# The first layer's normalization and routing moved in front of the first round of a two-layer recurrent block

## The chip, the cores and the metric

The kernel runs on one core of a Trainium2 chip. The metric is the time of one execution on the device in microseconds (us), median of several runs. The core has a matrix engine (TensorE, PE in the profile), a vector engine (VectorE, DVE), an activation engine (ScalarE, ACT), a general engine (GpSimd, POOL), a queue that issues most transfers (SyncE, SP) and 16 DMA engines. Each engine works through its own list of instructions in order and waits on semaphores for the others. Data lies in SBUF, a memory of 128 partitions; matmul results go to the eight banks of PSUM.

## The reference

x has two sequences of 2048 tokens of 256 numbers. There are two layers, each of the form x + s * silu(g), where s is an attention branch and g a feed-forward branch, both of them computed from the layer-normalized x:

```python
xn = _layernorm(x, axis=-1)
s = _L0_attn_ref(xn, ...)            # local attention of 16 heads, window 128, and 64 pooled latent tokens
g = _silu(_L0_ffn_ref(xn, ...))      # mixture of 8 experts
x = x + s * g
xn = _layernorm(x, axis=-1)
s = _L1_attn_ref(xn, ...)            # a second transformer block
g = _silu(_L1_ffn_ref(xn, ...))      # two layers of rotary local attention with a gated feed-forward
x = x + s * g
```

Only the first layer is touched here, and of it mostly the choice of expert:

```python
router_logits = x @ Wr.T                                   # 4096 x 8
expert_idx = jnp.argmax(jax.nn.softmax(router_logits, axis=-1), axis=-1)
for e in range(E):                                         # E = 8
    mask = (expert_idx == e)[:, None].astype(x.dtype)
    inter = inter + mask * gelu(x @ W1[e] + b1[e])         # 256 -> 1024
y = inter @ Wo + bo + x                                    # 1024 -> 256
out = layernorm(y) * gamma + beta
```

So each token goes to exactly one expert, the one with the largest of its eight logits.

## The kernel before

Tokens lie in 32 tiles of 128, and four tiles make a group, so there are eight groups (`NT` = 32, `GT` = 4, `NG` = 8). Everything is fp32.

**The first layer runs in eight rounds**, one for each group. A round is the attention of its four tiles. Beside it run the projections of the next group (`head(g + 1)`: queries, keys, latent queries and latent keys) and a share of the experts. The function `in_turn` merges such pieces: each piece (a lane) is a list of steps with weights and is given a stretch of the round, (0.05, 0.75) for instance; the steps of all lanes are sorted by their place and issued in that order. The engines keep the order in which the instructions were issued, so this list is the order of work on each engine.

**Normalization and logits: `prep(g)`.** For each tile of the group two DVE instructions find mean and variance (L79, L80). POOL turns them into 1/sqrt(var + eps) (L84, L85). DVE normalizes the four tiles in place (L88). SP stores the rows to DRAM, to `rows_n` (L916), from where the experts will gather them. TensorE transposes the eight 128x128 pieces (L890), DVE and ACT copy the two halves to SBUF (L71, L69), and eight matmuls against the 256x8 router weights give the logits of the four tiles (L898, two passes each). DVE then finds the largest of eight logits for each token as a one-hot row, in five small instructions (L906 to L910). Groups 0 to 3 go in front of round 0, together with `head(0)`; groups 4 to 7 run as lanes inside round 0. The buffers of x are four, so the loads of groups 4 to 7 wait for earlier stores.

**Routing: `route()`**, at 0.48 to 0.6 of round 0. The experts work on tokens sorted by expert, in 39 tiles of 128 places (`FT` = 32 + 8 - 1), each of which belongs to one expert. Two matmuls give each token's rank inside its tile and each tile's count for each expert (L936). `running` sums the counts over the tiles by doubling, ten DVE instructions (L942 to L946). `ends` gives the number of tiles for each expert and their running sum (L955 to L969). `places_of` gives each token's place (L975 to L981), and `tiles_of` splits it into tile and row by comparing with all 40 tile edges (L987 to L995). `experts_of` gives the expert of each of the 39 tiles, as integers `exi` (L1030 to L1034). `tokens_of` inverts the map: for each of the eight groups DVE builds two one-hot operands, `one` and `num` (L1002 to L1013), and four matmuls add them up in one PSUM bank (L1016); from this come the token numbers of every place, `src` (L1024 to L1026).

**Experts.** SP reads each tile's expert number into a register (L1051) and loads that expert's 1 MB of weights, two tiles deep (L1054). POOL gathers the 128 rows of `rows_n` (L1056). TensorE transposes them (L1069), does the first product (L1083), ACT does Gelu (L1092), TensorE the second product with `Wo` (L1100). The result is normalized, scaled and stored sorted (L1115). The list of expert steps is dealt out to the rounds by `shares`: 0.35 for round 0, 1 for rounds 1 to 6, 0.03 for round 7. In round 0 the experts take the last 0.35. The load of `Wo` and of the bias rows and the first expert's weights and rows are issued after routing, when the memory of x is free (`open_experts`).

**Attention.** Scores of one block of 64 queries are made in four banks (L114); DVE adds the mask and finds the row minimum (L107), ACT takes exponentials (L136, and L1245 for the latent part), TensorE transposes (L151) and multiplies with the values (L165). The projections are L204 and L207, L208 (queries), L214, L218 and L220 (keys), L1171 (latent queries), L228 and L236 (values).

The second layer follows and overlaps with the last round; it is the larger part of the time and is not touched.

Of the kernel before, what the change touches and what calls it, by code (L numbers as in the profile page):

```python
# [8 lines left out]
AF = mybir.ActivationFunctionType  # L9
ALU = mybir.AluOpType  # L10
AX = mybir.AxisListType
# [19 lines left out]
def kernel(ctx: ExitStack, tc: tile.TileContext, io: dict, col: dict):  # L31
# [787 lines left out]
    with ExitStack() as l0_ctx:  # L819
# [11 lines left out]
        x_ctx = ExitStack()  # L831
        xp = pool("xp", 1, "right", x_ctx)
        xn = {}

        def load_x(g):
            if g < NG:
                xn[g] = sb(xp, [P, GT, D], "xn", 4)
                nc.sync.dma_start(xn[g], xin[:, g * GT : (g + 1) * GT, :])

        for g in range(4):  # L840
            load_x(g)
            if g == 0:
                wr = sb(l0, [P, 2, E], "wr")
                nc.sync.dma_start(wr, io["WrT"].rearrange("(k p) e -> p k e", p=P))
                wqkv = sb(wa, [P, 2, 3 * D], "wqkv")
                nc.sync.dma_start(wqkv, io["L0_attn_qkv_w"].rearrange("(k p) n -> p k n", p=P))
                rqw = sb(wa, [P, 2, 64], "rqw")
                nc.sync.dma_start(rqw, io["L0_attn_rq_w"].rearrange("(k p) n -> p k n", p=P))
                rkvw = sb(wa, [P, 2, 128], "rkvw")
                nc.sync.dma_start(rkvw, io["L0_attn_rkv_w"].rearrange("(k p) n -> p k n", p=P))  # L850
                halves = load_halves(wa, "halves_a")
            if g == 1:
                routw = sb(wa, [64, 2, P], "routw")
                nc.sync.dma_start(routw, io["a_rout_w"].rearrange("p (e n) -> p e n", e=2))
                outw = sb(wa, [P, 2, D], "outw")
                nc.sync.dma_start(outw, io["a_out_w"].rearrange("(k p) n -> p k n", p=P))
                rows = load_rows(wa, "rows_a")
        cst_a = sb(wa, [P, io["cst_a"].shape[1]], "cst_a")
        nc.sync.dma_start(cst_a, io["cst_a"])
# [4 lines left out]
        edges = cst_a[:, 648 : 649 + FT]  # L864
        starts = edges[:, 0:NT]
        places = cst_a[:, 649 + FT : 649 + 2 * FT]
        along, down = cst_a[:, 649 + 2 * FT : 777 + 2 * FT], cst_a[:, 777 + 2 * FT : 778 + 2 * FT]
# [6 lines left out]

        def prep(g):
# [3 lines left out]
            o = oh[:, g * GT : (g + 1) * GT, :]  # L879

            def moments(t):
                if not t:
                    d["mv"] = sb(xp, [P, GT, 2], "ln_mv", 3)
                    d["rs"] = sb(xp, [P, GT], "ln_rs", 3)
                ln_moments(xp, d["mv"], t, [xn[g][:, t, :]])

# [6 lines left out]
            def logits():  # L893

                lg = d["lg"] = bank("s")[:, 0 : GT * E].rearrange("p (t e) -> p t e", t=GT)
                for t in range(GT):
                    for k in range(2):
                        nc.tensor.matmul(  # L898
                            lg[:, t, :],
# [5 lines left out]
                mx = sb(xp, [P, GT], "mx", 2)  # L905
                nc.vector.tensor_reduce(mx, lg, AX.X, ALU.max)  # L906
                nc.vector.tensor_tensor(o, lg, bc(mx, 2, [P, GT, E]), ALU.is_equal)
                nc.vector.tensor_tensor(o, o, bc(desc, 1, [P, GT, E]), ALU.mult)
                nc.vector.tensor_reduce(mx, o, AX.X, ALU.max)
                nc.vector.tensor_tensor(o, o, bc(mx, 2, [P, GT, E]), ALU.is_equal)  # L910

            lane = [(1, lambda t=t: moments(t)) for t in range(GT)]
            lane += [(1, lambda: ln_rsqrt(d["rs"], d["mv"], 1e-5)), (2, lambda: None)]
            lane += [(1, lambda t=t: normalize(xn[g][:, t, :], xn[g][:, t, :], d["mv"], d["rs"], t)) for t in range(GT)]
            store = rows_n[g * GW : (g + 1) * GW, :].rearrange("(t p) d -> p t d", p=P)
            lane.append((0, lambda: nc.sync.dma_start(store, xn[g])))  # L916
            lane += [(1, lambda c=c: turn(c)) for c in range(2)] + [(1, lambda: None), (1, logits)]
            return lane + [(0, lambda: load_x(g + 4))]

        def route():  # L920

            d = {}
            flat = oh.rearrange("p t e -> p (t e)")

            def two(shape, tag):
                return [sb(xp, shape, f"{tag}{i}") for i in range(2)]

            def ranks():
                ones = sb(xp, [P, P], "ones")
                nc.vector.memset(ones, 1.0)  # L930

                d["rank"] = sb(xp, [P, NT, E], "rank")
                d["total"] = sb(xp, [P, NT, E], "total")
                for name, m in (("rank", before), ("total", ones)):
                    mm = bank("s")[:, 0 : NT * E]
                    nc.tensor.matmul(mm, lhsT=m, rhs=flat, start=True, stop=True)  # L936
                    nc.vector.tensor_copy(d[name].rearrange("p t e -> p (t e)"), mm)

            def running():

                cum = two([P, NT, E], "cum")
                nc.vector.tensor_copy(cum[0], d["total"])  # L942
                k, a = 1, 0
                while k < NT:
                    nc.vector.tensor_copy(cum[1 - a][:, 0:k, :], cum[a][:, 0:k, :])
                    nc.vector.tensor_tensor(  # L946
# [113 lines left out]
        def expert(i):  # L1060
            d = {}

            def begin():
                if i + 1 < FT:
                    expert_load(i + 1)
# [865 lines left out]
```

## Time and profile before

| | us |
|---|---|
| median of 3 runs (lowest, highest) | 2983.13 (2982.27, 2983.95) |
| the profiled execution | 2981.85 |
| its span, first to last instruction | 2980.1 |
| PE busy | 2745.5 (92%) |
| DVE busy | 1900.0 (64%) |
| ACT busy | 1676.8 (56%) |
| POOL busy | 1090.0 (37%) |

The mean clock granted to TensorE is 0.959 of full. In the tables below a row gives a stretch of the span, its length, then for each engine the us in which it was busy and, in brackets, the number of instructions; then the granted clock, the share of time in which the DMA engines were busy and the rate. PEld is the loading of weights into TensorE, which overlaps with its matmuls. In the timeline a row gives start, length, engine, line, operation, output and inputs, and in square brackets how long the engine was idle before it and what ended this. One fp32 matmul shows as two records.

### The profile page before, as it was taken

To read this page: it belongs to the slowest core of one execution; us is meant where nothing else is said; L and a number is where in the kernel's file an instruction comes from. 1 tells how busy PE (TensorE), PEld (TensorE's weight loads), DVE (VectorE), ACT (ScalarE), POOL (GpSimd) and SP (SyncE) were. 2 spreads that over 40 slices of the span, in tenths; PEclk is the share of its full clock that TensorE was granted. 3 is DMA by queue.
4 is the path that set the end of the run, shared out by engine and by line. 5 is a ranking of instruction groups with operands and counts; after the bars stand their busy time and mean duration, and the time that the engine had idled before them with its cause. 6 is when DMAs were issued, how large, how long until landed. Compare 5 with 4: busy or idle time off the path is not lost.

```text
span 2980.1 us, 72390 instructions
## 1 busy us (share of the span) xinstructions
PE 2745.5 (92%) x28226; PEld 1979.7 (66%) x28226; DVE 1900.0 (64%) x6725; ACT 1676.8 (56%) x4587; POOL 1090.0 (37%) x1236
## 2 busy tenths in 40 slices
PE   6789999999987899999999999999998999999997
PEld 4567787787864556656666666666666666666666
DVE  5746655565666877767676777676766555555542
ACT  2347777777764444544444444555554566777672
POOL 1113333333344555555453544443544112222212
PEclk7789999999988999999999999999999999999999
DMA  4032222222211111010000010000001010000000
GB/s 149 24 109 90 81 86 97 82 83 85 92 32 56 62 30 30 23 30 26 16 26 30 16 31 16 5 6 7 5 5 31 18 38 18 28 23 23 15 16 22
DMA packets 84229, 123.57 MB, mean 41 GB/s; under 512 B 7729, under 2 KB 74449, under 8 KB 78897
## 3 DMA queue, kind: packets, MB, share of 16 engines
q1 hardware_dynamic: 80480, 109.64, 11.3%
q0 software_dynamic: 3408, 9.31, 1.1%
q8 instruction: 224, 3.67, 0.5%
q14 instruction: 117, 0.95, 0.1%
HBM read 88.65 MB, written 21.89 MB: 37 GB/s over the span
## 4 chain that ended last, share of the span: by engine, by line
PE 64%; DVE 15%; ACT 11%; issue 5%; POOL 4%; DMA 1%; SPq 0%; POOLq 0%; DVEq 0%; ACTq 0%
PE s L744 10%; PE s L535 5%; PE s L766 4%; PE s L1100 4%; PE tp L151 4%; PE s L1083 3%; PE s L1725 3%; ACT pr L136 3%; PE s L663 3%; ACT pr L1598 3%; PE s L551 2%; PE s L1712 2%; DVE pr L107 2%; PE s L458 2%; PE acc L488 2%
## 5 line engine op out<-in xcount | busy, mean ns | idle before, releaser
L579 POOL TENSOR_TENSOR inv<-inv,nhalf 128x16 f32<-128x16 f32 x64 | 187.2, 2925 | 448.3 <-DVE inv L578 448.1
L107 DVE CUSTOM_DVE_ANT_0 pr<-s,cst 128x128 f32<-128x128 f32 (+2 forms) x1024 | 261.4, 315 | 95.8 <-PE s L1578 73.7
L478 ACT ACTIVATE pr<-pr,mn 128x192 f32<-128x192 f32 (+2 forms) x512 | 188.5, 439 | 237.1 <-DVE mn L107 216.8
L744 PE MATMUL s<-h2T,d_w 128*128 128x512 f32 x704 | 317.3, 603 | 0.4 <-ACT pr L478 0.4
L69 ACT COPY pt<-tp 128x384 f32<-128x384 f32 (+3 forms) x320 | 156.8, 495 | 253.4 <-PE tp L151 226.2
L136 ACT ACTIVATE pr<-pr,mn 128x192 f32<-128x192 f32 (+2 forms) x512 | 222.9, 437 | 67.7 <-DVE mn L107 67.3
L1598 ACT ACTIVATE pr<-pr,mn 128x128 f32<-128x128 f32 x512 | 198.1, 388 | 107.0 <-DVE mn L107 106.7
L71 DVE COPY pt<-tp 128x384 f32<-128x384 f32 (+3 forms) x320 | 181.3, 567 | 107.0 <-PE tp L151 77.6
L535 PE MATMUL s<-d_wqkv,hT 128*128 128x512 f32 x512 | 237.3, 605 | 0.0
L568 POOL TENSOR_TENSOR scr<-scr,tab 128x512 f32<-128x512 f32 x128 | 168.2, 1314 | 184.6 <-DVE scr L71 184.5
L744 PEld LDWEIGHTS s<-h2T,d_w 128*128 128x128 f32 x704 | 133.4, 193 | 153.3 <-issue 151.8
L151 PE MATMUL tp<-cst,pr 128*128 128x128 f32 x1488 | 214.8, 280 | 15.8 <-ACT pr L478 10.0
L151 PEld LDWEIGHTS tp<-cst,pr 128*128 128x128 f32 x1488 | 178.2, 144 | 55.7 <-issue 22.7
L757 DVE SCALAR_TENSOR_TENSOR u<-s,cols,ge 128x512 f32<-128x512 f32 x96 | 71.9, 749 | 204.6 <-PE s L744 124.2
L766 PE MATMUL s<-d_w,u 128*128 128x256 f32 x768 | 179.2, 383 | 0.0
L1730 POOL TENSOR_TENSOR x<-x,stream 128x256 f32<-128x256 f32 x32 | 23.3, 728 | 373.1 <-DVE x L1729 373.1
L766 PEld LDWEIGHTS s<-d_w,u 128*128 128x128 f32 x768 | 143.5, 191 | 23.9 <-issue 3.7
L165 PE MATMUL acc<-pt,v 64*32 64x128 f32 x4992 | 122.4, 287 | 37.2 <-DVE latT L1316 16.9
L1100 PE MATMUL s<-Wo,it 128*128 128x128 f32 x1248 | 155.7, 278 | 0.8 <-DVE mnl L107 0.8
L535 PEld LDWEIGHTS s<-d_wqkv,hT 128*128 128x128 f32 x512 | 93.9, 194 | 91.2 <-issue 90.9
L1100 PEld LDWEIGHTS s<-Wo,it 128*128 128x128 f32 x1248 | 146.4, 192 | 9.3 <-issue 7.8
L107 DVE CUSTOM_DVE_ANT_0 pr<-s,cst_a 128x192 f32<-128x192 f32 (+2 forms) x512 | 144.0, 347 | 11.6 <-PE s L114 8.7
(294 smaller groups left out, 6512.0 us busy)
## 6 DMA issues: line engine op xcount, KB each, us to landing
w<-in_W1b_dram SPq DMA_DIRECT2D x39, 1028.0 KB
ysort<-ys SPq DMA_DIRECT2D x39, 128.0 KB
xn<-in_L_attn_x_dram SPq DMA_DIRECT2D x8, 512.0 KB
rows_n<-xn SPq DMA_DIRECT2D x8, 512.0 KB
rows_s<-s SPq DMA_DIRECT2D x32, 128.0 KB
stream<-in_L_attn_x_dram SPq DMA_DIRECT2D x8, 512.0 KB
sg<-rows_s SPq DMA_DIRECT2D x8, 512.0 KB
rows_r<-stream SPq DMA_DIRECT2D x8, 512.0 KB
```

The source lines that it names most:

```text
L71: nc.vector.tensor_copy(out, in_)
L107: nc.vector.tensor_tensor_reduce(pr, sc, mask, 1.0, CAP, ALU.add, ALU.min, mn)
L136: nc.scalar.activation(w, w, AF.Exp, bias=mn[:, v : v + 1], scale=-1.0, accum_out=zs[:, v, blk, s : s + 1])
L151: nc.tensor.transpose(tp[:, k * P : (k + 1) * P], pr[:, k, :, :].rearrange("p v j -> p (v j)"), ident)
L478: nc.scalar.activation(p, p, AF.Exp, bias=mn[:, w : w + 1], scale=-1.0)
L535: nc.tensor.matmul(mm, lhsT=heads[r][:, k, t * P : (t + 1) * P], rhs=wqkv_d[l][:, k, j * INNER : (j + 1) * INNER], start=(k == 0), stop=(k ...
L568: nc.gpsimd.tensor_tensor(d["r2"][:, :, :, 32 * hf : 32 * hf + 32], d["qk"][:, :, :, 32 - 32 * hf : 64 - 32 * hf], bc(d["tab"][:, 2:4, hf, ...
L579: nc.gpsimd.tensor_tensor(inv.rearrange("p a h -> p (a h)"), inv.rearrange("p a h -> p (a h)"), nhalf, ALU.pow)
L744: nc.tensor.matmul(mm, lhsT=w1[l][:, k, c, :], rhs=d["h2T"][:, k, 0:w], start=(k == 0), stop=(k == 1))
L766: nc.tensor.matmul(mm[:, 0:D], lhsT=d["u"][:, c, i * P : (i + 1) * P], rhs=w2[l][:, c, :], start=(c == 0), stop=(c == HC - 1),)
L1100: nc.tensor.matmul(mm, lhsT=d["it"][:, ic, :], rhs=late["Wo"][:, ic, h], start=(ic == 0), stop=(ic == FF // P - 1))
L1598: nc.scalar.activation(w, w, AF.Exp, bias=mn[:, v : v + 1], scale=-1.0, accum_out=zs[:, v, blk, st : st + 1])
```

## The change

Five things are changed in the first layer.

- **All eight groups are normalized, transposed and given logits before round 0.** The eight buffers of x are loaded at the start, interleaved with the weights; `wr` comes first.
- **The normalization moves from DVE to ACT**, as x * rs + off. POOL makes `off` with two more instructions for each group.
- **The logits of all 32 tiles stand in one PSUM bank** (256 columns), and the one-hot rows are made in two halves of 16 tiles, five DVE instructions each, instead of once for each group.
- **The sums over tiles are matmuls.** Counts of each (tile, expert) pair come from two matmuls with a matrix of ones, and their running sums from matmuls with a 256x264 constant `cst_r` in place of the doubling on DVE. The tile of a place comes by rounding, in place of the comparison with 40 edges. One of the two `num` operands is scaled on ACT, and `num` has two buffers.
- **Routing stands in front of round 0**, merged with `head(0)` and the first scores, and **experts run in all rounds**: the first share is 1 instead of 0.35, and the experts' lane in round 0 begins at 0. The two loads of an expert are split: weights as soon as the expert numbers are there, rows when the token numbers are. `Wo` is loaded at the start.

```diff
+        cst_r = sb(ph, [P, GT, D], "sg", 1).rearrange("p t d -> p (t d)")[:, 0 : 2 * (NT * E + E)]
+        Wo = sb(l0, [P, FF // P, D], "Wo")
-        for g in range(4):
-            load_x(g)
+        for g in range(NG):
+            xn.append(sb(xp, [P, GT, D], "xn", NG))
+            nc.sync.dma_start(xn[g], xin[:, g * GT : (g + 1) * GT, :])
+            if g == 3:
...
...
+        logits = bank("acc")[:, 0 : NT * E].rearrange("p (t e) -> p t e", e=E)
...
+            def scales():
+                ln_rsqrt(d["rs"], d["mv"], 1e-5)
+                nc.gpsimd.tensor_tensor(d["off"], d["mv"][:, :, 0], d["rs"], ALU.mult)
+                nc.gpsimd.tensor_scalar(d["off"], d["off"], -1.0, 0.0, ALU.mult, ALU.add)
+
+            def norm(t):
+                x = xn[g][:, t, :]
+                nc.scalar.activation(x, x, AF.Identity, bias=d["off"][:, t : t + 1], scale=d["rs"][:, t : t + 1])
...
-            lane += [(1, lambda: ln_rsqrt(d["rs"], d["mv"], 1e-5)), (2, lambda: None)]
-            lane += [(1, lambda t=t: normalize(xn[g][:, t, :], xn[g][:, t, :], d["mv"], d["rs"], t)) for t in range(GT)]
+            lane += [(1, scales), (2, lambda: None)] + [(1, lambda t=t: norm(t)) for t in range(GT)]
...
+        def choose(half):
+            ts = slice(half * NT // 2, (half + 1) * NT // 2)
+            o, lg, shape = oh[:, ts, :], logits[:, ts, :], [P, NT // 2, E]
+            mx = sb(l0, [P, NT // 2], "mx", 2)
+            nc.vector.tensor_reduce(mx, lg, AX.X, ALU.max)
+            nc.vector.tensor_tensor(o, lg, bc(mx, 2, shape), ALU.is_equal)
+            nc.vector.tensor_tensor(o, o, bc(desc, 1, shape), ALU.mult)
+            nc.vector.tensor_reduce(mx, o, AX.X, ALU.max)
+            nc.vector.tensor_tensor(o, o, bc(mx, 2, shape), ALU.is_equal)
...
+            def counts():
+                mm = bank("s")[:, 0 : 2 * P]
+                for h in range(2):
+                    nc.tensor.matmul(
+                        mm[:, h * P : (h + 1) * P], lhsT=flat[:, h * P : (h + 1) * P], rhs=ones, start=True, stop=True
+                    )
+                d["cnt"] = sb(xr, [P, 2, P], "cnt")
+                nc.vector.tensor_copy(d["cnt"].rearrange("p h n -> p (h n)"), mm)
...
+                for h in range(2):
+                    nc.tensor.matmul(mm[:, 0:n], lhsT=d["cnt"][:, h, :], rhs=cst_r[:, h, 0:n], start=(h == 0), stop=False)
+                nc.tensor.matmul(mm[:, 0:n], lhsT=before, rhs=flat, start=False, stop=True)
+                for h in range(2):
+                    nc.tensor.matmul(
+                        mm[:, n : n + E], lhsT=d["cnt"][:, h, :], rhs=cst_r[:, h, n:], start=(h == 0), stop=(h == 1)
+                    )
+                nc.scalar.copy(d["rank"].rearrange("p t e -> p (t e)"), mm[:, 0:n])
+                nc.vector.tensor_copy(d["total"], mm[:, n : n + E])
...
-            def running():
...
-            def tiles_of():
...
+                nc.vector.tensor_scalar(f, at, 1.0 / P, -0.5 + 0.5 / P, ALU.mult, ALU.add)
+                nc.vector.tensor_scalar(f, f, 1.5 * 2.0**23, None, ALU.add)
+                nc.vector.tensor_scalar(f, f, -1.5 * 2.0**23, None, ALU.add)
+                nc.vector.tensor_scalar(p, f, -float(P), None, ALU.mult)
...
+                num = sb(xr, [P, GT, 2, FT], "num", 2)
+                here = num[:, :, 1, :]
+                nc.vector.tensor_tensor(
+                    here, bc(d["f"][:, ts], 2, [P, GT, FT]), bc(places, 1, [P, GT, FT]), ALU.is_equal
+                )
+                nc.vector.tensor_tensor(num[:, :, 0, :], here, bc(starts[:, ts], 2, [P, GT, FT]), ALU.mult)
+                nc.scalar.activation(here, here, AF.Copy, scale=down)
...
+            lane = [(1, lambda: choose(1))]
+            lane += [(1, f) for f in (counts, ranks, ends, experts_of, places_of)]
+            return lane + [(0.7, lambda g=g: tokens_of(g)) for g in range(NG)] + [(0.5, sources)]
...
+        def open_weights():
+            nonlocal pw
+            pw = pool("pw", 1, "right", right_ctx)
+            expert_weights(0)
...
-        in_turn(*((0.5 * g, 0.5 * g + 1, prep(g)) for g in range(4)), (0.9, 1.8, head(0)))
-        project_values(0)
-        score(0)
-        score(1)
+        in_turn(*((0.4 * g, 0.4 * g + 1.6, prep(g)) for g in range(NG)), (3, 3.1, [(1, lambda: choose(0))]))
+        ahead = [lambda: project_values(0), lambda: score(0), lambda: score(1)]
+        in_turn((0, 1, route()), (0.1, 0.6, head(0)), (0.75, 1.1, [(1, f) for f in ahead]))
...
-        shares = [0.35, 1, 1, 1, 1, 1, 1, 0.03]
+        shares = [1, 1, 1, 1, 1, 1, 1, 0.03]
...
-            if g == 0:
-                lanes += [(0.09 * k, 0.09 * k + 0.2, prep(4 + k)) for k in range(4)]
-                lanes += [(0.48, 0.6, route()), (0.6, 0.62, [(1, open_experts), (1, lambda: expert_load(0))])]
...
-                lanes.append((0 if g else 1 - shares[g], shares[g] if g == NG - 1 else 1, share))
+                lanes.append((0, shares[g] if g == NG - 1 else 1, share))
```

## The prediction

> **What bounds the kernel now.** I read the table of busy time by stretches of the span first, because the change touches only the first of the two layers, and then, inside the stretch that stands out, the timeline.
>
> ```profile
> core 0: us, PE busy (x) PEld busy (x) DVE busy (x) ACT busy (x) POOL busy (x), PEclk, DMA share, GB/s
> 0.00:60.00 60.00, 38.59 (x202) 27.68 (x202) 31.24 (x135) 14.33 (x53) 5.28 (x14) 0.81 0.54 176
> 60.00:132.00 72.00, 58.55 (x484) 42.39 (x482) 49.98 (x214) 28.79 (x107) 11.18 (x18) 0.71 0.10 32
> 132.00:177.00 45.00, 21.78 (x134) 17.82 (x134) 25.71 (x78) 6.08 (x27) 5.70 (x7) 0.54 0.17 56
> 177.00:500.00 323.00, 307.45 (x3745) 259.92 (x3745) 191.14 (x846) 240.96 (x803) 112.67 (x170) 1.00 0.26 90
> 500.00:865.00 365.00, 344.02 (x4163) 291.76 (x4163) 219.75 (x979) 266.49 (x893) 134.11 (x204) 0.99 0.25 82
> 865.00:1000.00 135.00, 100.09 (x1095) 65.50 (x1096) 90.53 (x315) 64.84 (x205) 62.05 (x65) 0.81 0.22 67
> ```
>
> The first expert's transposes run at 177.1 and the last expert tile is stored at 865. Between them TensorE is busy 651.5 of 688 us, 94.7%, at full clock: that stage is TensorE's. Before 177 nothing is: TensorE is busy 119 us, most of them at half clock, and summed by record with cold time halved this is only 76.4 us of full-clock work. So 100 us of the first 177 are slack, and the worst stretch is 132 to 177, where the routing of tokens runs alone on DVE:
>
> ```profile
> 128.50 0.62 PE L1270 MATMUL acc<-ptl,rv 64*32 64x256 f32 x4
> 129.05 0.93 PE L114 MATMUL s<-kT,q 32*128 32x192 f32 x16
> 129.80 0.35 PE L1224 MATMUL s<-rk,rq 32*128 32x64 f32 x8
> 140.32 1.88 PE L165 MATMUL acc<-pt,v 64*32 64x128 f32 x48 [10.17 <-DVE latT L1316]
> 142.13 1.12 PE L1322 MATMUL s<-routw,latT 64*64 64x128 f32 x8
> 147.28 1.97 PE L1016 MATMUL s<-num,one 128*128 128x78 f32 x8 [4.04 <-DVE num L1013]
> 149.87 2.00 PE L1016 MATMUL s<-num,one 128*128 128x78 f32 x8 [0.62 <-DVE num L1013]
> ```
>
> TensorE waits 10 us for a latent operation that queues on DVE behind the routing, then does the eight token groups one per 2.62 us. No expert can start before that, and the attention of round 0 has no expert work to fill its own gaps.
>
> **The change, as one sum.** All eight normalizations and the routing go in front of round 0, then rounds 0 to 7 are attention mixed with experts from the first tile. The end of the expert stage is then (start of round 0) + (TensorE work left) / (density of the mixed stage). I work out each.
>
> *Front, part 1: eight groups of normalization, transposes and logits.* The instruction orders of the two kernels give this order on TensorE: 8 transposes, then the logits of the same group, eight times, with nothing between. The last group of the kernel before is that very sequence:
>
> ```profile
> 41.95 2.25 PE L890 MATMUL tp<-cst,xn 128*128 128x128 f32 x8 [1.55 <-issue]
> 43.39 0.69 DVE L71 COPY stream<-tp 128x512 f32<-128x512 f32 x1 [0.57 <-PE tp L890]
> 44.13 3.90 PE L898 MATMUL s<-wr,stream 128*128 128x8 f32 x16
> 44.24 0.58 ACT L69 COPY stream<-tp 128x512 f32<-128x512 f32 x1 [7.35 <-PE tp L890]
> 47.97 2.03 PE L228 MATMUL s<-wqkv,stream 128*64 128x128 f32 x16
> ```
>
> From 41.95 to 47.97 is 6.0 us; with 0.1 to the next, 6.1 us a group at half clock. The other engines fit below that: DVE 4 moments at 0.53 (pitch of L79 with L80) and a copy of 0.69 are 2.8 us; ACT 4 normalizations and a copy of 0.58. The ACT normalization (128x256, scale and bias by partition) is not in the trace; it lies between the 128x256 copy (0.38) and the 128x256 activation out of PSUM at L1179 (0.56). I take 0.5, so ACT has 2.6 us a group (2.8 at the upper end). The two new POOL operations (0.19 to 0.3 each) make POOL 1.9 us. All are hidden by TensorE at 6.1; at full clock the group would be 0.9 of transposes, 0.6 of copy and latencies of 0.4, and 1.75 of logits (L898 at 28.4), 3.6 or a little less, and ACT would still fit. Loads: x comes at 1.7 us a group (1.65 MB landed between 6.2 and 11.2), ahead of either.
>
> First group: x is issued 0.5 us later than before (wr goes ahead of it), so moments run 6.6 to 8.8, POOL to 11.1 (its two extra operations), four normalizations to 13.1, the second half of the transposes to 14.2. ACT has two normalizations of group 1 queued ahead of the copy (x1 and POOL ready near 13.1), so the copy ends at 15.1 and the logits at 18.7. Seven more groups at 6.1: **61.4**. The argmax of the first half (five operations on DVE) falls into this and costs at most 1.5 if TensorE's writes to the shared logits bank wait for it; I take 0.6. **62**.
>
> *Front, part 2: from the last logits to the first expert.* On DVE and TensorE, in their order, us after 62:
> - argmax of the second half: 5 operations on 128x128, between 0.19 (L906, 32 elements) and 0.42 (256), 0.3 each: 1.5.
> - counts matmul 0.6 and its copy 0.42 with latencies: to 2.7. Rank matmuls, eight records of 0.2 to 0.43 cold and two more passes of 0.43: to 6.1. These replace the running sums (L942 to L946, 124.9 to 127.6, 2.7 us), so the matmul form saves nothing when cold.
> - DVE then has both query projections in its queue ahead of the tile counts. They wait for TensorE (q0 at 0.86 a record, 3.4; q1 half warm, 2.4), ACT 0.78, DVE 0.81: 14.0.
> - tile counts 2.15 (128.11 to 130.26), key copy 0.75, experts 1.4 (143.81 to 145.23): the expert numbers are there at 18.4. Places: two 256-element products at 0.43 to 0.83, a reduction of 0.45, six small ones at 0.2, 2.7; latent query 0.54. This skips tiles_of, 4.8 us (134.64 to 139.4).
> - first token group 1.1 on DVE and 0.4 on ACT: 23.1. Then TensorE: two buffers instead of one for num let it run groups back to back, 2.0 cold, 1.1 (DVE's pitch: 0.62, 0.24, 0.24) once warm. Three cold, four warm, plus latent keys, values and score(0): 37.4.
> - the last token group stands behind score(0) on ACT: 12 exponentials at a pitch of 0.33, 4.0, and 0.8: 42.1; TensorE cold again 2.0; three DVE operations 0.85: 45. Gather 0.9 to its issue and 3.0 to landing: **49**.
>
> So the first expert starts at 111 instead of 177.1. Bounds for part 2: from above the whole old route with attention in it, 120.7 to 177.1, 56 us (118); from below the chain without the two queues (query 7.9, exponentials 4.4) and with a warm clock, 33 (95).
>
> SP: the eight stores wait for ACT, the last at about 57, before anything reads them. Weights for two experts are issued right behind the expert numbers (near 82), 25 us early. The other 37 reads of expert numbers, 0.56 each, 21 us, stand ahead of the bias rows (L276); they end near 103, and those rows cannot be issued before 107 anyway. POOL's first bias add waits for them (109 to 110): no cost below 111. The new constant, 270 KB, and the early Wo land by 30. I cost these at nothing.
>
> *Work left.* By line, of the 76.4 us done before 177, the front now holds 10.4 (L890), 14.3 (L898), 7.9 (L1016), 7.1 (half of L204 and L214), about 1.7 of counts and ranks and 4 of the first latent, value and score steps: 45.4. So 31.0 us of attention of round 0 and projections of group 1 come on top of the 651.5: 682.5.
>
> *Density.* At 94.7% the extra 31 take 32.7 us. The mixed stage has 39 expert tiles over 28 attention tiles instead of about 25, so less to fill gaps with. Without experts a tile still takes 20 to 25 us (value biases at L236 from 857 to 923); with 24.4 us of TensorE work a tile it has little room. I take 94.3%: 3.0 us more.
>
> Sum: 177.1 - 111 - 32.7 - 3.0 = **30.4 us** earlier. What follows 865 keeps its instructions. The profiled execution took 2981.85 (span 2980.1 and 1.75 around it), 1.28 below the median of 2983.13; against that median the forecast is 2983.1 - 30.4 = **2953**.
>
> **The page that would have it otherwise.** From 36.8 to 40.2 the logits kept TensorE busy 3.36 of 3.4 us and the clock stayed at half:
>
> ```profile
> 36.80:40.20 3.40, 3.36 (x16) 3.39 (x16) 0.00 (x0) 0.09 (x1) 0.57 (x1) 0.50 0.42 129
> ```
>
> The Trainium skill, "TensorE: Matmul & The Clock Gate", section "What's actually happening", has the clock go full after about 3.4 us of sustained activity; by that rule a front that is busy 5 of every 6 us would be warm. The row says that 8-column logits do not count as activity; the 512-column projections that followed at 18.9 did bring the clock up, at 23.1.
>
> **Rivals.**
> 1. *Warm front*: the clock rises in part 1. Groups take 3.6 us, the last logits end at 18 + 25 = 43.5 and everything comes 18 us earlier: 2935. For it: dense transposes in every group; against it: the row above, and 36.8 to 74.3 all at half clock.
> 2. *Density drops somewhat*: the attention chain, DVE and ACT in order, shows through with fewer experts beside it. At 92.5% the stage is 682.5 / 0.925 - 682.5 / 0.943 = 14 us longer: 2967. For it: the 20 to 25 us a tile; against: ACT at 74% and DVE at 60% have room.
> 3. *Slower*: the same mechanism past its tipping point. At 682.5 / (865 - 111) = 90.5% the gain is gone; at 89.5%, 2991. The tiles without experts, 865 to 1000, ran at 74%, which shows the direction; that a tenth fewer experts costs over four points is unlikely.
> 4. *Nothing gained*: the reordered front is as long as the old one, first expert near 142 with the same work left. It needs 30 us that no row shows.
>
> **How the numbers follow.** Forecast (front 95 to 118, density 93.5 to 94.7%, 2938 to 2962, middle 2953): 0.60. Warm front (2928 to 2938): 0.14. Some density lost (2962 to 2976): 0.14. Slower (2990): 0.07. Nothing gained: 0.05. 0.2% is 6 us, about what three runs within 1.7 us can tell with a rebuilt kernel. Leaving out the slower cases, the empty one and the ends of the outer two, the range is 2932 to 2974. Faster 0.88, same 0.05, slower 0.07.
>
> **What would show it.** First group of logits ending near 18.7 and then 6.1 us a group at half clock (3.6: rival 1); argmax of the second half at 62; query projections ahead of the tile counts on DVE; eight exponentials ahead of the last token group on ACT; first expert transposes near 111; TensorE 94% busy from there to the last expert's store near 835. Wrong would be a first expert after 125, or under 92% in the mixed stage.

## The result, and the profile after

The changed kernel takes 2976.9 us (median of 11 runs, 2966.26 to 2981.66); the kernel before took 2985.2 beside it (11 runs, 2980.86 to 2990.89). The ratio is 0.9965, 95% interval 0.9951 to 0.9978, so the change saves 7 to 15 us. The forecast was 30 us, and the time lies outside its range of 2932 to 2974. The profiled execution after the change took 2966.26 us, the lowest of the eleven; it was granted a mean clock of 0.970, the ones near the median 0.962 to 0.964, so its stretches are read here, not its total.

The stretches of the changed kernel, in the columns used before:

```profile
core 0: us, PE busy (x) PEld busy (x) DVE busy (x) ACT busy (x) POOL busy (x), PEclk, DMA share, GB/s
0.00:59.00 59.00, 44.66 (x193) 40.41 (x193) 23.58 (x82) 21.94 (x41) 13.44 (x39) 1.00 0.71 233
59.00:113.00 54.00, 34.39 (x177) 26.39 (x176) 26.14 (x108) 14.04 (x55) 2.16 (x2) 0.66 0.15 54
...
113.00:853.50 740.50, 695.07 (x8368) 581.58 (x8368) 446.29 (x1985) 540.11 (x1828) 256.45 (x388) 0.98 0.23 78
```

And the mixed stage of the kernel before, from its first expert to its last expert store, cut at the same two events:

```profile
177.10:864.70 687.60, 651.48 (x7908) 551.68 (x7908) 410.62 (x1824) 507.45 (x1695) 246.68 (x374) 0.99 0.26 86
```

The first expert's transposes now run at 113.1 instead of 177.1: 64.0 us earlier. The last expert tile is stored at 853.5 instead of 864.7: only 11.2 us earlier. The mixed stage between them grew from 687.5 to 740.4 us, by 52.9. So the front gave what was hoped for, and the stage behind it took four fifths of that back.

**The front came as worked out.** The timeline of TensorE in part 1 of the changed kernel (start, length, operation; 193 instructions in 59 us):

```profile
20.04 3.90 PE L906 MATMUL acc<-wr,stream 128*128 128x8 f32 x16
23.80 1.95 PE L900 MATMUL tp<-cst,xn 128*128 128x128 f32 x8
25.68 3.90 PE L906 MATMUL acc<-wr,stream 128*128 128x8 f32 x16
29.43 1.95 PE L900 MATMUL tp<-cst,xn 128*128 128x128 f32 x8
```

Eight transposes take 1.95 us and sixteen logit records 3.90, both at half the pace that transposes reach elsewhere (1.09 us for eight in run 7 below). (The clock column shows 1.00 in the first stretch because the trace holds no record of the clock before 65.5; the durations tell it.) A group comes every 5.6 us, in these rows with no idle time between; once, where the argmax of the first half stands, TensorE waits 1.6 us. The last logits end at 59.1. Then VectorE in part 2:

```profile
60.41 0.29 DVE L929 TENSOR_TENSOR oh<-oh,mx 128x128 f32<-128x128 f32 x1
...
70.13 0.81 DVE L208 TENSOR_SCALAR q<-s,cols,bqo 128x512 f32<-128x512 f32 x1 [0.91 <-ACT q L207]
...
74.82 0.18 DVE L993 CAST exi<-ex 128x39 int32<-128x39 f32 x1
...
96.62 0.32 DVE L1027 TENSOR_TENSOR num<-num,cst_a 128x156 f32<-128x156 f32 x1
...
101.56 0.23 DVE L107 CUSTOM_DVE_ANT_0 pr<-s,cst_a 128x64 f32<-128x64 f32 x1 [4.61 <-PE s L1246]
```

The argmax of the second half ends at 60.7, both query projections stand ahead of the tile counts, and the expert numbers are there at 75.0. After 96.9 VectorE goes through the first scores, and the last token group comes behind their exponentials; `src` is there at 109.0.

**The mixed stage by waits.** TensorE's longest waits between first expert and last store, changed kernel (who waited for whom, us in total, times, longest):

```profile
PE s L261 <- ACT oT L254: 11.9, 14, 1.8
PE s L114 <- ACT it L1114: 8.7, 13, 1.9
PE acc L165 <- DVE pt L71: 8.6, 7, 2.2
PE s L114 <- DVE xsT L1093: 4.2, 2, 2.6
```

The same of the kernel before, over its own stage:

```profile
PE s L261 <- ACT oT L254: 12.2, 14, 1.7
PE acc L165 <- DVE pt L71: 10.0, 9, 2.0
...
PE s L114 <- ACT it L1092: 2.3, 5, 0.5
PE s L114 <- DVE xsT L1071: 1.7, 1, 1.7
```

Most of the longest waits are alike; those of attention's scores (L114) for the experts' operands (`it` on ACT, `xsT` on DVE) grew from 4.0 to 12.9 us. TensorE's idle time in the stage rose from 36.1 to 45.3. That is 9.2 of the 52.9. The other 43.6 us are busy time, of which 7.0 are half-clock time (half of what was busy at half clock: 6.4 before, 13.4 after) and 36.6 are work.

### The profile page after: what moved, and what is told of

The parts are those of the page before. It is cut to its first block, busy times and chain, and to the rows that moved or that the text cites. A ratio compares the mean times of both kernels' runs of the same rounds, so it can differ in the third digit from the quotient of the medians.

```text
span 2964.5 us, 72419 instructions
## 1 busy us (share of the span) xinstructions
PE 2742.2 (93%) x28236; PEld 1984.9 (67%) x28236; DVE 1877.6 (63%) x6649; ACT 1696.4 (57%) x4628; POOL 1094.2 (37%) x1253
## 4 chain that ended last, share of the span: by engine, by line
PE 62%; DVE 15%; ACT 13%; issue 6%; POOL 4%; DMA 1%; SPq 0%; POOLq 0%; DVEq 0%; ACTq 0%
PE s L744 10%; PE s L535 5%; PE s L766 4%; PE s L1122 3%; ACT pr L136 3%; PE tp L151 3%; PE s L663 3%; PE s L551 2%; PE s L1743 2%; PE s L1105 2%; ACT pr L1616 2%; PE s L1730 2%; PE s L458 2%; DVE pr L107 2%; PE acc L488 2%
## 5 line engine op out<-in xcount | busy, mean ns | idle before, releaser
L107 DVE CUSTOM_DVE_ANT_0 pr<-s,cst_a 128x192 f32<-128x192 f32 (+2 forms) x512 | 144.0, 347 | 18.2 <-PE s L114 12.6
L1105 PE MATMUL s<-xsT,w 128*128 128x128 f32 x1248 | 148.7, 278 | 0.2 <-DVE xsT L1093 0.2
```

Of the source, the lines that this page charges most:

```text
L107: nc.vector.tensor_tensor_reduce(pr, sc, mask, 1.0, CAP, ALU.add, ALU.min, mn)
L1105: nc.tensor.matmul(mm[:, c * P : (c + 1) * P], lhsT=w[:, k * FF + ic * P : k * FF + (ic + 1) * P], rhs=d["xsT"][:, k, :], start=(k == 0), ...
```

## The experiments

Each run is compared with runs of the kernel before on the same chip, because chips differ: the second layer, which no kernel here touches, took 2111 to 2115 us after the last expert store on the chip of the result and 2092 to 2097 on the others. The letters in the expectations are names of theories, with what each expects beside it. The two that mattered: that the stage is TensorE's and the experts were late or too sparse, so that where the experts start, or how they are spread, decides its end; and (D in the later ones) that an attention tile has a price of its own in time, and that an expert tile adds a fixed price to it wherever it is put. All edits are to the changed kernel unless another is named.

**1. The experts of round 0 back to the last third, all else as changed.**

```diff
-        shares = [1, 1, 1, 1, 1, 1, 1, 0.03]
+        shares = [0.35, 1, 1, 1, 1, 1, 1, 0.03]
...
-                lanes.append((0, shares[g] if g == NG - 1 else 1, share))
+                lanes.append((0 if g else 1 - shares[g], shares[g] if g == NG - 1 else 1, share))
```

> The changed kernel with one part undone: the experts take the last 0.35 of round 0 with a share of 0.35, as before; normalization and routing stay in front. Theory A (each attention tile has a nearly fixed amount of TensorE waiting, set by the order of ACT and DVE, so thinner expert work does not shorten a tile in proportion): rounds 1 to 6 go back to about 107 us each with 6.1 experts, the tiles of round 0 without experts take about 21 to 22 us for 17 us of TensorE work, and the time is 2 to 10 us above the changed kernel, 2975 to 2985. Theory B (TensorE works through its list at a fixed share of the time, and the loss is half-clock stretches that fall by chance): within 4 us of the changed kernel, either way, and no relation between experts for a tile and TensorE idle.

Measured: 2950.28 us, ratio to before 0.9949 (0.993 to 0.9969). Its first expert runs at 157.5, 44 us later than in the changed kernel, and its last expert tile is stored at 854.8, against 853.5 and, in the repeat below, 854.6. Its stretches before and after the first expert:

```profile
113.00:157.00 44.00, 37.78 (x456) 24.52 (x455) 29.98 (x150) 29.41 (x117) 6.45 (x9) 0.88 0.02 4
157.00:855.00 698.00, 660.87 (x7914) 560.33 (x7912) 413.30 (x1837) 511.26 (x1712) 249.52 (x377) 0.98 0.25 83
```

Round 0 takes 101.0 us with 3 experts instead of 122.1 with 6, and rounds 1 to 6 take 652.4 us with 36 experts instead of 629.7 with 33. So "experts in all rounds" is worth nothing: three expert tiles cost some 21 us of round 0 and 23 of the later ones, 7.0 and 7.6 us a tile. That the experts start 44 us earlier doesn't show in the end at all. By its ratio this run even gained more than the changed kernel did on two other chips (0.9965 and, in the repeat below, 0.9987); the changed kernel was not run on this chip, so whether late experts are better is not shown.

**2 and 3. No Gelu table.** The Gelu is left out, so ScalarE has no table to switch. In the second of these the same edit is made to the kernel before.

```diff
-                            it[:, ic, :], mm[:, c * P : (c + 1) * P], AF.Gelu, bias=w[:, 2 * FF + ic : 2 * FF + ic + 1]
+                            it[:, ic, :], mm[:, c * P : (c + 1) * P], AF.Identity, bias=w[:, 2 * FF + ic : 2 * FF + ic + 1]
```

> The changed kernel with Identity in place of the experts' Gelu (the Gelu is left out), so that ACT loads no table between exponentials and Gelu: 78 loads of 1.28 us, 100 us of ACT, go; TensorE work is the same. Theory A, with ACT's order as what holds TensorE up: the stage from the first to the last expert (740 us) gets 12 us or more shorter, half-clock stretches in it become rarer, time about 2950 to 2962. Theory B: under 5 us, since TensorE has the same work and its waits are not ACT's.

> The kernel before with the same replacement (the Gelu is left out). Theory A: it gains as well, but less than the changed kernel does, since its expert work is denser and hides more: 2970 to 2980, so that the distance to the changed kernel with the same replacement grows from 8 to 10 us to about 20. Theory B: the distance stays at 8 to 10.

Measured: 2923.43 us (ratio 0.9861, 0.9842 to 0.9881) and 2940.97 (0.9928, 0.991 to 0.9947). The mixed stages of the two, from first expert to last store:

```profile
113.60:824.80 711.20, 684.19 (x8368) 574.23 (x8368) 445.18 (x1983) 441.43 (x1750) 256.32 (x388) 0.99 0.25 82
```

```profile
171.20:838.80 667.60, 644.35 (x7908) 546.93 (x7908) 408.86 (x1824) 408.57 (x1617) 246.86 (x374) 0.99 0.26 88
```

Without ScalarE's switches between Gelu and exponential (78 table loads of 1.28 us in this stage, in both kernels) the mixed stage of the changed kernel is 711.2 us, 29 less, and TensorE is busy 684.2 of them, 96.2% instead of 93.9%; that of the kernel before is 667.6 us, 20 less. Not one TensorE instruction was taken away. So 93.9% was not TensorE at its limit: a stage can look full and still follow another engine. Without the switches the change is worth 17.5 us by the medians, more than the 8.3 with them, though on another chip; by the last expert store it is 14.0 us (838.8 to 824.8) against 11.2.

**4 and 5. No expert products.** The experts' transposes, both products and Gelu are left out, and with them VectorE's copies and sums of their results; their loads, gathers, normalization and stores stay; first in the changed kernel, then in the kernel before.

```diff
-                tp = bank("tp")
-                for k in range(2):
-                    nc.tensor.transpose(tp[:, k * P : (k + 1) * P], d["xs"][:, k * P : (k + 1) * P], ident)
...
-                w = d["w"]
-                it = d["it"] = sb(pm[0], [P, FF // P, P], "it", 2)
-                for half in range(2):
...
-                mm = bank("s")[:, 0:P]
-                for ic in range(FF // P):
...
-                nc.vector.tensor_tensor(y[:, h], mm, y[:, h], ALU.add)
```

> The changed kernel without the experts' transposes, products and Gelu (left out; the weights, the gather and the normalization of the sorted rows stay): the attention's own pace. Theory A: an attention tile still takes 20 us or more in rounds 1 to 6 for about 16 us of TensorE work, because ACT and DVE in their order need that. Theory B: 17 to 18 us, TensorE's own work at its usual share.

> The kernel before without the experts' transposes, products and Gelu (left out as in the run on the changed kernel without them). Theory D (two terms: an attention tile costs about 20 us by its own chain and an expert tile 4.6 us in its gaps, and the two add up): rounds 1 to 6 at 80 us as there, and the last attention tile of the first layer (value bias of tile 31, at 733 us there) 10 to 14 us later, 743 to 747: the change's gain is there without any expert work. Theory E (the gain of 30 us was there and was eaten by the thinner mix of experts): without experts the full gain shows, tile 31 at 760 or later.

Rounds 1 to 6 of the stripped changed kernel, and below it of the stripped kernel before:

```profile
188.00:669.00 481.00, 402.60 (x4982) 280.46 (x4980) 348.86 (x1602) 303.85 (x1232) 223.92 (x341) 0.86 0.18 61
```

```profile
194.50:686.00 491.50, 407.50 (x4984) 281.06 (x4984) 351.56 (x1612) 305.00 (x1234) 232.86 (x356) 0.84 0.32 109
```

This is the pair that settles most. Six rounds of attention without any expert product take 481 us in the changed kernel, 80.2 a round, 20.0 us a tile (491 us and 81.9 a round in the kernel before), with no engine full: TensorE is busy 84% (part of it at half clock), VectorE 73%, ScalarE 63%. The full-clock TensorE work of such a tile is 14 us (388.6 us over 27 to 28 tiles, from 129.7 to 675.5). With 5.5 experts beside them the same rounds take 105.0 in the changed kernel:

```profile
216.00:846.00 630.00, 592.36 (x7189) 495.72 (x7188) 382.90 (x1706) 462.02 (x1571) 223.40 (x338) 0.99 0.24 79
```

So an expert tile costs on average (105.0 - 80.2) / 5.5 = 4.5 us of time, its table switches included, for 7.5 us of TensorE work ((681.7 - 388.6) / 39), much of it in the gaps of attention; and an attention tile alone costs 20 us for 14. In these two kernels the change brings the start of round 7 from 686 to 669: 17 us, with no expert products to be given back. Only 6 of them are there at the start of round 1 (194.5 to 188.2). The other 10 arise in rounds 1 to 6, with 157 us at half clock in the kernel before and 136 in the changed one; why they differ is not known. In the stripped kernel before the values of tile 31 come at 749.1 (733.1 in the changed one), between the 743 to 747 of theory D and the 760 of theory E, nearer to D.

**6. Dense first, thin later**: all but a few experts in rounds 0 to 3.

```diff
-        shares = [1, 1, 1, 1, 1, 1, 1, 0.03]
+        shares = [1.5, 1.5, 1.5, 1.5, 0.35, 0.35, 0.3, 0.03]
```

> The changed kernel with the same 39 expert tiles dealt out unevenly: shares 1.5 for rounds 0 to 3, 0.35 for 4 to 6: about 2.1 expert tiles for an attention tile and then 0.5. Theory D: dense tiles near 29.5 us, thin tiles 22 us (20 + 0.5 * 4.6), where TensorE's work alone would be 18.5; if the terms add up without a limit the end of the experts stays within 5 us of the changed kernel's; TensorE's own work in the dense tiles, 13.9 + 2.1 * 7.65 = 30 us, is the limit that may bend this, then dense tiles are 31 to 32 us and the whole 15 to 30 us later. Theory B (a fixed share of TensorE's time): dense 31.5, thin 18.5, sum unchanged.

Measured: 2966.73 us, ratio 1.0024 (1.0014 to 1.0034). The first and the last of the three dense rounds after round 0, and the three thin ones:

```profile
232.00:350.00 118.00, 116.54 (x1388) 101.48 (x1386) 70.03 (x303) 86.17 (x288) 47.16 (x73) 1.00 0.33 113
467.60:596.00 128.40, 122.21 (x1400) 105.98 (x1399) 66.62 (x300) 89.78 (x290) 46.55 (x70) 0.97 0.27 92
596.00:865.00 269.00, 234.61 (x2842) 177.70 (x2842) 170.38 (x788) 178.10 (x672) 66.69 (x104) 0.90 0.11 34
```

With these the time of a round can be set against the experts in it:

| experts in a round | us a round | from |
|---|---|---|
| 0 | 80.2 | changed, no products, rounds 1 to 6 |
| 0 | 81.9 | before, no products, rounds 1 to 6 |
| 1.67 | 89.7 | this run, rounds 4 to 6 |
| 5.5 | 105.0 | changed, rounds 1 to 6 |
| 6.0 | 107.7 | before, rounds 1 to 6 |
| 6.0 | 108.7 | run 1, rounds 1 to 6 |
| 8.33 | 121.4 | this run, rounds 1 to 3 |

From 0 to 6 the points lie within 2 us of a line, 80.2 + 4.55 an expert (87.8 where 89.7 was measured). The line gives an average price: from 5.5 to 6 experts a round the step is steeper, 17 us (before against changed) to 23 us (run 1) for three experts, 5.5 to 7.6 each, and 7.6 is about an expert's own TensorE work. Of the dense rounds the first two take 118.0 us each with TensorE busy 99%, which is on the line (118.1). The third, with TensorE busy 95%, takes 128.4, and these 10 us are the larger part of what this run loses (last store 870.5 against 854.6 in the repeat below). So a full TensorE doesn't explain the loss, and what slows the third round isn't shown.

**7. Dense logits.** The router matmul is turned round: the weights are stationary and 512 tokens move past them, so that the 8x512 result has to be copied and transposed back in four small pieces.

```diff
+                mm = bank("s")[0:E, :]
+                for k in range(2):
+                    nc.tensor.matmul(mm, lhsT=wr[:, k, :], rhs=xT[:, k, :], start=(k == 0), stop=(k == 1))
+                lt = d["lt"] = sb(xp, [P, GW], "lt", 2)[0:E, :]
+                copy(g, lt, mm)
+
+            def spread():
...
-                    for k in range(2):
-                        nc.tensor.matmul(
-                            logits[:, g * GT + t, :],
-                            lhsT=xT[:, k, t * P : (t + 1) * P],
...
+                    nc.tensor.transpose(logits[:, g * GT + t, :], d["lt"][:, t * P : (t + 1) * P], ident[0:E, 0:E])
...
-        in_turn(*((0.4 * g, 0.4 * g + 1.6, prep(g)) for g in range(NG)), (3, 3.1, [(1, lambda: choose(0))]))
+        in_turn(*((0.4 * g, 0.4 * g + 2.03, prep(g)) for g in range(NG)), (3.4, 3.5, [(1, lambda: choose(0))]))
```

> The changed kernel with the logits of a group made the other way round: router weights stationary (8 columns), 512 tokens moving, two matmuls a group, a copy, and four small transposes a step later. That the front runs at half clock because 8-column matmuls do not count as activity (theory of the prediction): the clock rises in the front, a group takes about 3.6 to 4 us instead of 5.6, the first expert starts 10 to 16 us earlier, near 100, and the time falls by as much against the changed kernel. If the clock stays at half all the same, a group takes 5 to 6 us and the time is the same.

The timeline of TensorE in its front, one group:

```profile
21.91 1.09 PE L900 MATMUL tp<-cst,xn 128*128 128x128 f32 x8
23.35 1.88 PE L906 MATMUL s<-stream,wr 128*8 128x512 f32 x4 [0.35 <-DVE stream L71]
25.17 0.41 PE L912 MATMUL acc<-cst,lt 8*128 8x8 f32 x4
25.51 1.09 PE L900 MATMUL tp<-cst,xn 128*128 128x128 f32 x8
```

Eight transposes now take 1.09 us instead of 1.95: the clock is full. A group takes 3.6 us instead of 5.6, the last logits end at 44.6 instead of 58.9, the first expert runs at 97.8 instead of 113.0, and the last store comes at 843.8 instead of 854.6. So 10.8 of the 15.2 us gained at the first expert are left at the last store: the stage has the same 27.9 attention tiles and takes 746.0 us instead of 741.6, with 46.0 us at half clock instead of 34.5. Measured: 2939.88 us, ratio 0.9931 (0.991 to 0.9953), and 16.3 us under the unedited changed kernel of the next paragraph. This version beats both kernels, and it is the warm front of the prediction's first rival (15 us earlier where the rival had 18), got by other means.

**The changed kernel again**, unedited, as the base for the two above.

> The changed kernel again, unedited, as the yardstick beside the next three. All theories: first expert's transposes near 113, last expert stored near 853, 8 to 15 us faster than the kernel before of this call.

Measured: 2956.16 us, ratio 0.9987 (0.9978 to 0.9997), with the same landmarks (last logits 58.9, first expert 113.0, last store 854.6) but 34.5 us at half clock in the stage instead of 27.5. So on this chip the change is worth 1 to 7 us, less than the 8 to 15 expected. How much of the 11 us survives depends on the chip; on both the gain is there and under half of the forecast.

**8. Routing inside round 0** (built on 7): attention starts right behind the logits, routing runs beside it, experts in the last part of the round.

```diff
-        ahead = [lambda: project_values(0), lambda: score(0), lambda: score(1)]
-        in_turn((0, 1, route()), (0.1, 0.6, head(0)), (0.75, 1.1, [(1, f) for f in ahead]))
+        in_turn((0, 1, head(0)))
+        project_values(0)
...
-        shares = [1, 1, 1, 1, 1, 1, 1, 0.03]
+        shares = [0.4, 1, 1, 1, 1, 1, 1, 0.03]
...
+            if g == 0:
+                lanes.append((0, 0.55, route()))
```

> The kernel with the dense logits (e7), with routing taken out of the front again: head(0) and the first scores follow the logits at once, the attention of round 0 begins, routing runs as a lane in the first 0.55 of round 0, and the experts take the last part of it with a share of 0.4. Theory D (attention tiles at 20 us and expert tiles at 4.6 us add up wherever the experts are put, so what counts is when the attention starts): values of tile 0 near 62 instead of 79, first expert only near 130 to 150, and still round 7 begins (values of tile 28) near 824 instead of 836 with routing's own 15 us in it; about 10 us faster than e7, 2930 on that chip. Theory F (what counts is when the experts start): round 7 begins 15 us or more later than in e7 and the time is 2955 or more.

Measured: 2942.52 us, ratio 0.994 (0.9916 to 0.9964). Its stretches around the routing:

```profile
50.00:100.00 50.00, 30.10 (x335) 22.19 (x334) 31.26 (x169) 27.39 (x124) 4.19 (x7) 0.72 0.11 44
100.00:150.00 50.00, 31.51 (x179) 22.93 (x179) 16.97 (x52) 9.92 (x30) 1.45 (x2) 0.64 0.01 3
150.00:200.00 50.00, 46.74 (x597) 38.70 (x596) 31.23 (x139) 38.34 (x132) 14.79 (x21) 0.99 0.26 82
```

The values of tile 0 are there at 54 instead of 79, 25 us earlier than in the seventh run, but tiles 1 to 2 and 2 to 3 then take 54 and 37 us, and tile 4 is only 6 us ahead (196 against 202). Nothing is full while routing runs (from 100 to 150, 32 of 50 us on TensorE and 17 on VectorE): it is a chain, and it costs attention about as much beside it as in front of it. The first expert runs at 159.2, 61 us later than in the seventh run, and the last store comes 2.3 us later. That rejects theory F, that the start of the experts sets the end; but D's 2930 was missed as well, as it had routing hide.

**9. Normalization on VectorE again**, without the two extra operations on POOL.

```diff
-                nc.gpsimd.tensor_tensor(d["off"], d["mv"][:, :, 0], d["rs"], ALU.mult)
-                nc.gpsimd.tensor_scalar(d["off"], d["off"], -1.0, 0.0, ALU.mult, ALU.add)
...
-                nc.scalar.activation(x, x, AF.Identity, bias=d["off"][:, t : t + 1], scale=d["rs"][:, t : t + 1])
+                normalize(x, x, d["mv"], d["rs"], t)
```

> The changed kernel with one part undone: the normalization in the front on DVE again, without POOL's two extra operations. A group then has 4.3 us of DVE work, still under the 5.6 us that its transposes and logits take on TensorE at half clock: logits of group 7 end within 2 us of 59, and the time is that of the changed kernel within 3 us. If ACT's normalization was what paid, the front ends 5 us or more later.

Measured: 2955.64 us, ratio 0.9976 (0.9964 to 0.9988). Last logits 60.2, last store 856.0, against 58.9 and 854.6: 1.3 us. Neither engine bounds the front; TensorE does.

## Why the prediction was wrong

**Front, part 1: right.** First group's logits forecast at 18.7, measured 18.3; 6.1 us a group, measured 5.6; last logits 62 with the argmax, measured 59.1. ACT's normalization takes 0.59 us, above the 0.5 taken, and stays hidden. The clock stayed at half, as the row of 8-column logits had said. The Trainium skill, "TensorE: Matmul & The Clock Gate", section "What's actually happening", would have had it rise after a few us of sustained activity. Here TensorE ran transposes and 8-column logits without idle time from 20 to 33 us and stayed at half clock, and with 512-column logits it was at full clock at 22, in less busy time. As far as these runs show, the rule holds here only if narrow matmuls are left out of activity.

**Front, part 2: right in its sum, in part by luck.** Expert numbers 80 forecast, 75.0 measured; `src` 107, measured 109.0; first expert 111, measured 113.1. So 5 us won at first were lost again: from expert numbers to `src` the forecast had 27 us, the trace 34.0. It had put four of the eight token groups at 1.1 us each on a warm clock, and the clock is at half from 75.8 to 116.7; two groups take 3.70 us there. The two queues that were costed, the queries ahead of the tile counts and the exponentials ahead of the last token group, both show. The 39 reads of expert numbers (75.0 to 98.6) and the stores cost nothing.

**"Work left" failed.** The forecast put TensorE busy at 682.5 us in the stage; it was 695.1. Of the 12.6 us that were missing, 7.0 are half-clock stretches, which went from 13.3 to 27.5 us and were not in the forecast. The other 5.6 are work: 36.6 us more in full-clock terms instead of 31.0. The front had indeed left 32.8 undone (76.4 before, 43.6 after); 3.8 the two traces differ by elsewhere, about as much as busy time moves when only ScalarE's work changes (681.7 to 676.5 in run 2), since the ends of matmuls are modelled.

**"Density" failed too, in the direction of the second rival.** 93.9% instead of 94.3%: 45.3 us idle instead of 41.3, 4.0 more. Together: 30.4 - 2.1 (front) - 12.6 - 4.0 = 11.7, where 11.2 was measured.

**What lies behind both**, as far as the runs show, is that the stage was priced as a heap of TensorE work at one density. The 94.7% was an average over two kinds of work with very different prices: 20.0 us of time for the 14 us of TensorE work in an attention tile alone, and on average 4.5 us for the 7.5 us in an expert tile. The change moves only attention. From the values of each tile the trace counts 25.4 attention tiles in the stage before and 27.9 after, with 39 experts in both. These 2.5 tiles took 52.9 us, where the forecast took 35.7; at 20.05 us each they would take 50. The row for it was in the prediction, as the 20 to 25 us that a tile takes without experts; it was used to doubt the density and not as a price.

How far do the two prices carry? At 39 x 4.55 + tiles x 20.05 the stages come to 687 and 737 us, where 687.5 and 740.4 were measured. These are near by construction, since the prices come from their rounds. Runs 1 and 8 have 25.9 and 25.6 tiles, so 697 and 691, and 697.3 and 686.8 were measured. Two runs don't fit: run 7 with 27.9 tiles (737 by the rule, 746.0 measured) and run 6 with 27.8 (735 and 757.5). And the price of an expert is not fixed, as run 1 shows (7.0 to 7.6 us). So the prices are a rough rule for stages mixed like these, not a law.

Part of an attention tile's price in the mix is ScalarE's table switches. Without them (runs 2 and 3, 27.9 and 25.4 tiles, both on another chip than the two profiles compared above) the change lengthens the stage by 43.6 us instead of 52.9, for nearly the same TensorE work (36.3 us in full-clock terms instead of 36.6); what idle time adds falls from 9.2 to 3.8 us, and what half clock adds from 7.0 to 3.5.

**The other parts.** Experts in round 0 bring nothing (run 1), since they add up with attention there as they do later. ACT's normalization is worth 1.3 us (run 9). What the change does gain is there at the start of round 1: with the experts placed as before, in run 1, tile 4's values come at 195 instead of 211. Which part of the new front brings it was not separated. That routing stands in front of attention is not it alone, since run 8, with routing inside round 0 again, stores its last expert only 2.3 us later than run 7. Rounds 1 to 6, with 36 experts in both, then give 6 of these 16 us back (652.4 us instead of 646.3), with 27 us at half clock instead of 10.

**What stays open.** That the moved work cost more than its share is measured; why is not settled. What binds an attention tile at 20 us isn't shown: in the run without products no engine is full, and TensorE, ScalarE and VectorE wait on one another in turn, at half clock in 150 of 546 us. The clock is steadier with experts (17 us at half clock in rounds 1 to 6 of the changed kernel, 136 in the same rounds without products), which may be part of why an expert is cheap; this was not separated. Nor is it known why the half-clock stretches grew, or why the chips differ.

## What to carry to other kernels

Where two kinds of work are interleaved in engines that run in order, don't price a moved piece by its busy time over the stage's mean density: take one kind out, run it alone, and read the price of each as the slope, time per tile against tiles per round. Read the slope also near the mix that you run: here it was 4.5 us an expert on average and up to 7.6 for the last three. An engine at 94% is not shown to be the bound until work of another engine is taken away and the time stays; here removing table loads alone gave 29 us. And a start that comes 64 us earlier is worth only what the piece that is now done later would have cost in its new place.

## What was not expected of the hardware

- In the front the clock went with the form of the logits matmuls and not with how busy TensorE was. With 8-column logits TensorE was busy 27.8 of the 30 us from 20 to 50 and the transposes took 1.95 us; with 512-column ones it was busy 25.4 of 30, and they took 1.09. Whether the columns or the number of weight loads matter was not separated.
- 78 table loads of 1.28 us, 100 us of ScalarE time in a stage where ScalarE was busy 73%, cost 29 us of the changed kernel's end (853.5 to 824.8) and 26 us of that of the kernel before (864.7 to 838.8), though with the runs on different chips.
- The same untouched second layer takes 2111 to 2115 us on one chip and 2092 to 2097 on three others, 0.7 to 1.1%, which is more than the change is worth; and the worth of the change itself was 0.35% on one chip and 0.13% on another.
